# Row additions up to eight chunks ahead of their scatters, five indirect transfers under way, and gathered chunks turned sooner in the plan

## The chip, the cores and the metric

The kernel runs on one core of a Trainium2 chip. Its time is the device time of one execution in microseconds (us); the kernel before takes 2306.5 us, the median of three runs (2304.06 to 2307.6). A core has engines that run their own queues in order and wait for each other by semaphores: PE (matrix products and transposes), DVE (elementwise work, reductions and statistics), ACT (activations, copies and scalings), POOL (here the indirect transfers), and SP (here only the issue of plain transfers). Transfers of all queues are carried by 16 DMA engines.

## The reference

The input x is 32 images of 128 channels, 56 by 56 pixels (3136 tokens of 128 numbers). Cut to what matters:

```python
# layer 0: group norm, sign, a 3x3 convolution with signs as weights
x = x + conv(sign(group_norm(x)), sign(w)) * alpha
# layer 1, on tokens t = x as (image, token, channel)
n = layer_norm(t)
kv = sum over tokens of (n @ Wk + bk) * (n @ Wv + bv)
t = t + (n @ Wq + bq) * kv
# a mixture of 8 experts, the best two of each token
n = layer_norm(t)
p = softmax(n @ router_w + router_b);  top_p, top_i = top_k(p, 2);  top_p = top_p / sum(top_p)
t = t + sum over the two of top_p * (n @ expert_w[top_i] + expert_b[top_i])
```

## The kernel before

An image has 25 chunks of 128 tokens (the last of 64), in 7 blocks of four (the last of one). For each image, PE makes the convolution (`conv`, L608), DVE adds it to x (`conv_add`), PE turns chunks to tokens (`to_tokens`, L635) and ACT copies them to SBUF (`to_tokens_out`, L645, into a `tok` buffer of which there are three). DVE takes statistics, ACT scales (`scaled`), PE sums the products that give kv (`gram`), and PE projects three chunks at a time (`project`, L831), which ACT scales out of PSUM (`project_out`, L845: three multiplications and a copy) and DVE adds (`project_add`). Then DVE routes each token to two experts.

The experts are applied in two ways. The first 8 or 12 chunks of an image (`DENSE`), and all 25 of the last four images, go through all eight experts: SP loads gates spread over all partitions (`spread`, L1101, tiles `bc` and `gt`), DVE multiplies (`gated`, L1116), PE applies the experts (`experts`, L1127), DVE adds, and SP stores. The other chunks of 28 images, in four groups of 8, 8, 8 and 4 images, are sorted by the pair of experts that a token uses, 428 chunks in all:

- `row_add` (L1330, ACT) adds a number to each row of a chunk in place, and `scatter` (L1337, POOL) writes the chunk's rows by an indirect transfer to their places in a table in DRAM, `rows`.
- When all scatters of a group are through, `tile_load` (L1627, SP) loads four tiles of 128 rows at a time, `tile_turn` (PE) turns them, `tile_turned` (ACT) copies them, `tile_experts` (L1647, PE) applies two experts to each, `tile_read` (L1665, ACT) scales the results out of PSUM, two tiles a step by four activations, DVE adds (`tile_sum`, `tile_out`), and `tile_store` (SP) writes them to a table `res` in DRAM.
- When a group's `res` is complete, `gather` (L1411, POOL) fetches each chunk's rows by an indirect transfer into one of 14 `back` buffers, `back_turn` (L1424, PE) turns the gathered chunks of a block, up to four at once, which frees their buffers, `back_out` (ACT) copies them and `back_store` (SP) stores them.

A group's scatters take place while the group before is being gathered; both use POOL's queue.

**What sets the order.** The kernel is written as steps. Each step has a due time, an engine, an estimate of its work in us, the steps that it comes after, buffers of rings that it takes or frees, and a `delay` until its result has landed (`at`, L463). `in_order` (L108) walks through a model of the engines in time: of the steps that could start first on an engine, it takes the one due first, and so writes one order of all steps. A step that takes a place in a ring, such as `("sent", ...)`, waits in the plan until the step that frees the place is done. The sizes of the rings are in `ROOM` (L90): `back` has 12 places in the plan; `sent` has no buffer behind it, and only bounds how many row additions stand ahead of their scatters in the plan. None of these figures is an instruction on the chip: they change the order in which the queues of PE, DVE and ACT are written, and these three are held to the planner's order (`IN_ORDER`, L72). SP and POOL are not: the scheduler that follows arranges their instructions by its own readiness model, in an order near the planner's.

Indirect transfers have one wait of their own. `in_turn` (L1489) makes each wait for one that came some places before it in the planner's order, whether scatter or gather:

```python
before = moved[-IN_FLIGHT:][:1] if len(moved) >= IN_FLIGHT else []
for b in before:
    tc.add_manual_dep(dma.ins, b.name, in_turn_dep, reason="few under way")
```

`GATHER_LANDS` is the delay that the plan gives to a gather, so it sets how long after the gathers `back_turn` stands in PE's order. The figures beside `project_out` and `tile_read` are the plan's estimates of ACT's work.

Of the kernel before, what the change touches and what calls it, by code (L numbers as in the profile page):

```python
# [70 lines left out]

IN_ORDER = {mybir.EngineType.PE, mybir.EngineType.DVE, mybir.EngineType.Activation}  # L72
NEWTON = 3
IN_FLIGHT = 4

GATE_LANDS, SPREAD_LANDS, STORE_LANDS, TILE_LANDS, GATHER_LANDS = 5.0, 6.5, 5.0, 6.0, 12.0
TILE_PACE = (0.7, 0.6, 0.4, 0.3)
GATHER_PACE = (1.0, 0.8, 0.5, 0.4)
N_Q = C + 2 * N_EXP
# [9 lines left out]
BANKS, EMPTIES = ("ps", "acc", "ff"), 7.0  # L89
ROOM = dict(  # L90
    x=3, tok=3, ps=5, acc=1, ff=2, y=3, qs=3, tt=4, bc=4, gt=2, gated=2,
    t_in=3, turned=2, v=3, w=2, back=12, sent=4, o=2,
)


# [82 lines left out]
def conv_attn_moe_kernel(  # L178
# [32 lines left out]
    def cols_of(b):  # L211
        return blocks[b][0] * C, min(n_tok, (blocks[b][-1] + 1) * C)
# [250 lines left out]
    def at(due, key, engine, work, do, *args, after=(), take=(), free=(), delay=0.0, slack=0.0):  # L463


        if isinstance(work, float):
            steps[key] = Step(due, key, engine, work, do, args, after, take, free, delay, slack, 0.0)
            return
        running = []

        def go_on():
            if not running:
                running.append(do(*args))
            next(running[0], None)

        lag = LAG if isinstance(work, list) else 0.0
        for j, w in enumerate(work):
            last = j == len(work) - 1
            part = key if last else (*key, "part", j)
            steps[part] = Step(  # L480
                due, part, engine, w, go_on, (), [(*key, "part", j - 1)] if j else after,
                [] if j else take, free if last else [], delay if last else 0.0, slack, lag,
            )

    def base(i):

        n = len(group_of)
        return P * (min(i, n) + 1.2 * max(0, i - n))
# [42 lines left out]
    def plan_image(i: int):  # L531
        s = base(i)
# [144 lines left out]
        for g in range(n_blk):  # L677
            b = min(n_conv - 1, (cols_of(g)[1] - 1) // (ROWS * width))
            due = s + 4 + 5.5 * b
            share = len(blocks[g]) / PER  # L680
# [109 lines left out]
        for g in range(n_blk):  # L790
            share = len(blocks[g]) / PER
# [28 lines left out]
        for g in range(n_blk):  # L820
            share = len(blocks[g]) / PER
# [50 lines left out]
        for j, cs in enumerate(q_groups):  # L872
            share = len(cs) / Q_GROUP
            biased = [("bias", i, g) for g in {cs[0] // PER, cs[-1] // PER}]
            at(
                s + 85 + 3.5 * j, ("project", i, j), "PE", 0.75 * share, project, j,
                after=[("kv_8", i), ("project", i, j - 1)] + biased, take=["ps"],
                free=[("x", ("load", i))] if j == last_q else [],
            )
            at(  # L880
                s + 86 + 3.5 * j, ("project_out", i, j), "ACT", 0.92 * share, project_out, j,
                after=[("project", i, j)], take=["qs"], free=[("ps", ("project", i, j))],
            )
            at(
                s + 87 + 3.5 * j, ("project_add", i, j), "DVE", (0.58 * share,) + (0.19,) * len(cs), project_add, j,
                after=[
                    ("project_out", i, j), ("route_1", i - 2), ("row_scalars", i - 2),
                    ("var2", i - 2),
                ],
                free=[("qs", ("project_out", i, j))],  # L890
            )
# [267 lines left out]
        for b in dense_blocks:  # L1159
            share = (cols_of(b)[1] - cols_of(b)[0]) / WIDE  # L1160
# [285 lines left out]
        due = begin + each * (i - last_of[group] + GROUPS[group] - 1)  # L1446
# [6 lines left out]
        for b in range(n_dense // PER, n_blk):  # L1453
            share = len(blocks[b]) / PER
# [34 lines left out]
    def in_turn(dma):  # L1489

        before = moved[-IN_FLIGHT:][:1] if len(moved) >= IN_FLIGHT else []
        for b in before:
# [7 lines left out]
    def parts_of(g):  # L1500
        return -(-quads_of(g) * PER // C)

    def quads_of(g):
        return -(-tiles_of(g) // PER)

    def tiles_due(g):

        return base(last_of[g]) + 195, TILE_PACE[g] * P * GROUPS[g] / quads_of(g)
# [192 lines left out]
    def plan_group(g):  # L1701
        last = last_of[g]
        s = base(last)
        at(
            s + 140, ("list_1", g), "DVE", [0.2, 0.2, 0.1, 0.1, 0.1, 0.1], list_1, g,
            after=[("count_on", last), ("list_3", g - 1, parts_of(g - 1) - 1), ("pad", g - 1, 6)],
        )
        at(s + 141, ("list_sum", g), "PE", 0.2, list_sum, g, after=[("list_1", g)], take=["ps"])
        at(
            s + 142, ("list_2", g), "DVE",  # L1710
            [0.1, 0.1] + [w * parts_of(g) for w in (0.25, 0.1, 0.2, 0.2, 0.18, 0.1)], list_2, g,
            after=[("list_sum", g)], free=[("ps", ("list_sum", g))],
        )
        for h in range(parts_of(g)):
            at(
                s + 143 + h, ("list_3", g, h), "PE", 0.25, list_3, g, h,
                after=[("list_2", g), ("list_4", g, h - 1)], take=["ps"],
            )
            at(
                s + 143.5 + h, ("list_4", g, h), "DVE", 0.25, list_4, g, h,  # L1720
                after=[("list_3", g, h)] + ([("tile_experts", g - 2, quads_of(g - 2) - 1, 0)] if g > 1 else []),
                free=[("ps", ("list_3", g, h))],
            )
        for j in range(7):
            at(
                s + 143 + 3 * j, ("pad", g, j), "SP", 1.6, pad, g, 4 * j, 4 * j + 4,
                after=[("list_1", g), ("open", g), ("pad", g, j - 1)], delay=3.0,
            )
        begin, each = tiles_due(g)
        members = [i for i in group_of if group_of[i] == g]  # L1730
        for q in range(quads_of(g)):
            due = begin + each * q
            at(
                due - 12, ("tile_load", g, q), "SP", 1.4, tile_load, g, q,
                after=[("list_4", g, parts_of(g) - 1), ("pad", g, 6)]
                + [("tile_load", g, q - 1) if q else ("tile_load", g - 1, quads_of(g - 1) - 1)]
                + [("scatter", i, c) for i in members for c in range(DENSE[g], n_ck)],
                take=["t_in"], delay=TILE_LANDS,
            )
            at(  # L1740
                due, ("tile_turn", g, q), "PE", 0.45, tile_turn, g, q,
                after=[("tile_load", g, q), ("tile_turn", g, q - 1), ("tile_experts", g, q - 2, 1)],
                take=["ps"],
            )
            at(
                due + 1, ("tile_turned", g, q), "ACT", 0.47, tile_turned, g, q,
                after=[("tile_turn", g, q)], take=["turned"], free=[("ps", ("tile_turn", g, q))], slack=1.0,
            )
            for h in range(2):
                at(  # L1750
                    due + 2 + 2 * h, ("tile_experts", g, q, h), "PE", 0.90, tile_experts, g, q, h,
                    after=[("tile_turned", g, q), ("tile_experts", g, q, h - 1)], take=["ps"],
                    free=[("turned", ("tile_turned", g, q))] if h else [],
                )
                at(
                    due + 3 + 2 * h, ("tile_read", g, q, h), "ACT", 1.40, tile_read, g, q, h,
                    after=[("tile_experts", g, q, h), ("tile_read", g, q, h - 1)],
                    take=[] if h else ["v", "w"], free=[("ps", ("tile_experts", g, q, h))], slack=2.0,
                )
            at(  # L1760
                due + 9, ("tile_sum", g, q), "DVE", 0.60, tile_sum, g, q,
                after=[("tile_read", g, q, 1)], free=[("w", ("tile_read", g, q, 0))],
            )
            at(
                due + 10, ("tile_out", g, q), "DVE", 0.61, tile_out, g, q,
                after=[("tile_sum", g, q), ("tile_out", g, q - 1)],
                free=[("t_in", ("tile_load", g, q))],
            )
            at(
                due + 12, ("tile_store", g, q), "SP", 0.35, tile_store, g, q,  # L1770
                after=[("tile_out", g, q), ("tile_store", g, q - 1)]
                + ([("gather", last_of[g - 2], n_ck - 1)] if q == 0 and g > 1 else []),
                free=[("v", ("tile_read", g, q, 0))], delay=STORE_LANDS,
            )

    for i in range(n_img):
        plan_image(i)
    for g in range(len(GROUPS)):
        plan_group(g)
# [67 lines left out]
```

## Time and profile before

| | |
|---|---|
| time, median of three runs | 2306.5 us (2304.06 to 2307.6) |
| the profiled execution's own time | 2298.39 us |
| its span, first to last instruction | 2296.5 us |
| mean granted clock of PE | 0.965 |
| PE busy | 2116.7 us, 92% |
| DVE busy | 1981.4 us, 86% |
| ACT busy | 1529.2 us, 67% |
| POOL busy | 1014.6 us, 44% |
| scatters, L1339 | 428, 1174 ns each; 758.2 us idle before them |
| gathers, L1414 | 428, 1149 ns each; 501.4 us idle before them |

By the trace, the scatters of group 0 are issued from 119 to 500 us, of group 1 from 531 to 1024, of group 2 from 1037 to 1616 and of group 3 from 1636 to 1930. Gathers begin at 883 us, and the last is issued at 2280 us.

The profile is of one execution. A group's line names the source line, the engine, the operation, the tile written and the tiles read, how often, the busy time and the mean, and the idle time of the engine just before with what ended it. An idle time is put down to the semaphore that changed last before it ended, which can name an instruction that the waiting one has nothing to do with, when the wait was for several things. SPq and the like are an engine's queue. A row of the table by stretches holds, after the stretch and its length, the busy time (and instructions) of PE, PE's weight loads, DVE, ACT and POOL, then PE's granted clock as a share of full speed, the share of time in which the DMA engines were busy, and GB/s.

### The profile page before, as it was taken

Reading aid. Unit: us, or ns where it says so; the run is one execution under the profiler, and the core shown is the slowest. Engines: PE = TensorE matmul, PEld = TensorE weight load, DVE = VectorE, ACT = ScalarE, POOL = GpSimd, SP = SyncE. Lnnn points to the kernel's source line nnn. Section 1 sums busy time; section 2 is a strip of 40 time slices with the busy share of each in tenths; the row PEclk is TensorE's granted clock in tenths of the full one; section 3 lists DMA queues with packets and bytes.
Section 4 is the critical chain, followed back from the end, with each engine's and each line's share of the span. In section 5 each row is a group of like instructions: output and inputs, shape, how many; then the busy total and the mean of one; then the engine's idle time right before and its main releaser. Section 6 shows DMA issues by size and latency. Waiting matters only on the chain.

```text
span 2296.5 us, 45166 instructions
## 1 busy us (share of the span) xinstructions
PE 2116.7 (92%) x12074; PEld 1454.8 (63%) x12074; DVE 1981.4 (86%) x6370; ACT 1529.2 (67%) x4885; POOL 1014.6 (44%) x991
## 2 busy tenths in 40 slices
PE   4989999999999999898999999999789989999989
PEld 2656556566777776566767766656567765666644
DVE  4899999999999999897789899899678868778885
ACT  5767767668788987477868877455567856674311
POOL 3044434334332225544555545545545455424564
PEclk9999999999999999899999999999899989999999
DMA  4054554455555655547767866566667766877798
GB/s 168 29 162 156 167 173 145 134 182 181 189 162 179 183 186 163 162 152 247 208 198 236 250 191 216 180 209 216 208 184 219 243 186 197 259 232 239 235 298 293
DMA packets 316010, 448.56 MB, mean 195 GB/s; under 512 B 60904, under 2 KB 221200, under 8 KB 315760
## 3 DMA queue, kind: packets, MB, share of 16 engines
q1 hardware_dynamic: 286032, 382.79, 52.5%
q0 software_dynamic: 28144, 56.14, 8.0%
q10 hardware_dynamic: 1584, 6.75, 0.8%
q8 instruction: 102, 1.67, 0.3%
q14 instruction: 148, 1.21, 0.2%
HBM read 319.51 MB, written 126.00 MB: 194 GB/s over the span
## 4 chain that ended last, share of the span: by engine, by line
PE 49%; DVE 29%; DMA 7%; issue 6%; ACT 4%; SPq 2%; another core or an unknown queue 2%; POOL 1%; DVEq 0%; ACTq 0%; POOLq 0%
PE ff L1137 16%; PE cv L615 9%; PE to L1656 7%; DVE gated L1119 6%; PE gram L717 4%; PE q L836 4%; DVE st L870 3%; DVE st L655 3%; DVE tok L788 3%; DVE tok L862 2%; DMA bc<-gp 2%; DMA t_in<-rows 2%; DVE x L626 2%; PE turn L1638 2%; PE xt L642 2%
## 5 line engine op out<-in xcount | busy, mean ns | idle before, releaser
L1339 POOL DMA_INDIRECT rows<-tok,row_no x428 | 502.3, 1174 | 758.2 <-ACT tok L1333 418.4
L1137 PE MATMUL ff<-gated,ew_d 128*128 128x512 f32 (+1 forms) x1536 | 721.6, 599 | 35.0 <-DVE gated L1119 28.1
L1414 POOL DMA_INDIRECT back<-res,res_no x428 | 491.8, 1149 | 501.4 <-PE back_ps L1429 154.4
L1119 DVE TENSOR_TENSOR gated<-tt,bc 128x1024 f32<-128x1024 f32 x384 | 450.4, 1178 | 91.0 <-PE ff L1137 43.5
L1137 PEld LDWEIGHTS ff<-gated,ew_d 128*128 128x128 f32 x1536 | 277.4, 195 | 277.5 <-issue 209.9
L615 PE MATMUL cv<-xs,w_bin 128*128 128x440 bf16 (+3 forms) x2016 | 424.3, 360 | 17.9 <-ACT xs L578 10.0
L1674 ACT ACTIVATE v<-to,t_in 128x128 f32<-128x128 f32 x528 | 253.9, 481 | 129.2 <-PE to L1656 59.7
L615 PEld LDWEIGHTS <-w_bin 128*128 128x128 bf16 x2016 | 199.9, 100 | 193.4 <-issue 41.7
L850 ACT ACTIVATE qs<-q,r 128x136 f32<-128x136 f32 (+1 forms) x800 | 246.6, 407 | 63.9 <-PE q L836 36.7
L1656 PEld LDWEIGHTS to<-ew_s,turned 128*128 128x128 f32 x2112 | 258.7, 193 | 38.0 <-issue 21.9
L1656 PE MATMUL to<-ew_s,turned 128*128 x2112 | 271.3, 278 | 8.0 <-issue 2.5
L708 ACT ACTIVATE y<-tok,r 128x128 f32<-128x128 f32 (+1 forms) x800 | 253.7, 414 | 35.3 <-DVE r L522 15.2
L836 PE MATMUL q<-move,x 128*128 128x144 f32 (+1 forms) x1600 | 242.0, 298 | 11.3 <-issue 3.0
L836 PEld LDWEIGHTS q<-move,x 128*128 128x128 f32 (+1 forms) x1600 | 215.6, 195 | 42.7 <-issue 16.7
L717 PEld LDWEIGHTS gram<-y 128*128 128x128 f32 (+1 forms) x1600 | 196.7, 191 | 33.7 <-issue 23.8
L655 DVE BATCH_NORM_STATS2 st<-tok 128x6 f32<-128x128 f32 (+1 forms) x800 | 178.4, 277 | 40.6 <-ACT tok L648 33.2
L717 PE MATMUL gram<-y 128*128 128x129 f32 (+1 forms) x1600 | 208.8, 276 | 0.0
L1681 ACT ACTIVATE w<-to,t_in 128x128 f32<-128x128 f32 x528 | 206.9, 392 | 0.0
L870 DVE BATCH_NORM_STATS2 st<-tok 128x6 f32<-128x128 f32 (+1 forms) x800 | 195.0, 281 | 0.0
L626 DVE SCALAR_TENSOR_TENSOR x<-cv,alpha_col,x 128x448 f32<-128x448 f32 x224 | 151.1, 675 | 44.7 <-PE cv L615 16.7
L648 ACT COPY tok<-xt 128x512 f32<-128x512 f32 (+1 forms) x224 | 117.2, 564 | 103.5 <-PE xt L642 56.2
L1333 ACT ACTIVATE tok<-tok,a 128x128 f32<-128x128 f32 (+1 forms) x428 | 171.8, 434 | 0.2
(228 smaller groups left out, 2908.6 us busy)
## 6 DMA issues: line engine op xcount, KB each, us to landing
bc<-gp SPq DMA_DIRECT2D x368, 512.0 KB
x<-in_x_dram SPq DMA_DIRECT2D x60, 784.0 KB
t_in<-rows SPq DMA_DIRECT2D x528, 66.0 KB
res<-v SPq DMA_DIRECT2D x132, 256.0 KB
out_dram<-o SPq DMA_DIRECT2D x100, 256.0 KB
out_dram<-tt SPq DMA_DIRECT2D x92, 256.0 KB
rows<-zeros SPq DMA_DIRECT2D x116, 66.0 KB
rows<-tok,row_no POOLq DMA_INDIRECT x428
```

Source lines behind the costliest of these rows:

```text
L615: nc.tensor.matmul(cv[:, r0:r1, c0:c1], lhsT=w_bin[:, t, :], rhs=xs[:, b * ROWS + dy + r0 : b * ROWS + dy + r1, dx + c0 : dx + c1], start= ...
L655: nc.vector.bn_stats(st[:n, c, :], d["tok"][:n, c, :C])
L708: nc.scalar.mul(y[:n, j, :C], d["tok"][:n, c, :C], d["r1"][:n, c : c + 1])
L717: nc.tensor.matmul(d["gram"], lhsT=y[:n, j, :C], rhs=y[:n, j, :], start=(c == 0), stop=(c == n_ck - 1),)
L836: nc.tensor.matmul(p[:n, k, :], lhsT=d["x"][:, c * C : c * C + n], rhs=move, start=True, stop=True,)
L870: nc.vector.bn_stats(st2[:n, c, :], d["tok"][:n, c, :C])
L1119: nc.vector.tensor_tensor(g[:, :, :n], d["tt", b][:, :n].unsqueeze(1).to_broadcast([C, 2, n]), d.pop(("bc", b, k))[:, :, :n], ALU.mult,)
L1137: nc.tensor.matmul(d["ff", b][:, :n], lhsT=ew_d[:, e * C : (e + 1) * C], rhs=g[:, j, :n], start=False, stop=(e == N_EXP - 1),)
L1339: dma = nc.gpsimd.indirect_dma_start(out=groups[group]["rows"], out_offset=bass.IndirectOffsetOnAxis(ap=d["row_no"][:n, c - n_dense : c - ...
L1414: dma = nc.gpsimd.indirect_dma_start(out=d["back", c][:n, :], out_offset=None, in_=groups[group]["res"][: quads_of(group) * WIDE, :], in_o ...
L1656: nc.tensor.matmul(p[:, k, j, :], lhsT=t[:, n * C : (n + 1) * C], rhs=ew_s[:, bass.ds(d["cols", q][j][n], C)], start=True, stop=True,)
L1674: nc.scalar.activation(d["v", q][:, n, :], p[:, k, 0, :], AF.Identity, bias=row[:, C + 2 : C + 3], scale=row[:, C : C + 1],)
```

## The change

Five figures change, and nothing else. The plan lets up to eight row additions stand ahead of their scatters, where it was four. Each indirect transfer waits for the fifth before it in the planner's order, where it was the fourth. The plan takes a gather to land after 9 us, where it was 12. It takes `project_out` for three chunks to need 0.84 us of ACT, where it was 0.92, and `tile_read` 1.20 us, where it was 1.40. The second is a wait on the chip; the others alter the order in which the steps are written.

```diff
-IN_FLIGHT = 4
+IN_FLIGHT = 5
-GATE_LANDS, SPREAD_LANDS, STORE_LANDS, TILE_LANDS, GATHER_LANDS = 5.0, 6.5, 5.0, 6.0, 12.0
+GATE_LANDS, SPREAD_LANDS, STORE_LANDS, TILE_LANDS, GATHER_LANDS = 5.0, 6.5, 5.0, 6.0, 9.0
...
 ROOM = dict(
     x=3, tok=3, ps=5, acc=1, ff=2, y=3, qs=3, tt=4, bc=4, gt=2, gated=2,
-    t_in=3, turned=2, v=3, w=2, back=12, sent=4, o=2,
+    t_in=3, turned=2, v=3, w=2, back=12, sent=8, o=2,
 )
...
-                s + 86 + 3.5 * j, ("project_out", i, j), "ACT", 0.92 * share, project_out, j,
+                s + 86 + 3.5 * j, ("project_out", i, j), "ACT", 0.84 * share, project_out, j,
...
-                    due + 3 + 2 * h, ("tile_read", g, q, h), "ACT", 1.40, tile_read, g, q, h,
+                    due + 3 + 2 * h, ("tile_read", g, q, h), "ACT", 1.20, tile_read, g, q, h,
```

## The prediction

> **What bounds the kernel now.** I read the page first, then the clock and busy time by stretch, then the waits of POOL, and last the order of time around the two worst stretches. The page's first part:
>
> ```profile
> span 2296.5 us, 45166 instructions
> PE 2116.7 (92%) x12074; PEld 1454.8 (63%) x12074; DVE 1981.4 (86%) x6370; ACT 1529.2 (67%) x4885; POOL 1014.6 (44%) x991
> ```
>
> PE is idle for 2296.5 - 2116.7 = 180 us, and that is all that a change of order can win, plus what a lower clock stretches. The table by stretches (length; busy time of each engine; then PE's granted clock, the DMA share, GB/s) says where:
>
> ```profile
> 1000.00:1060.00 60.00, 49.48 (x288) 33.76 (x287) 51.97 (x192) 35.16 (x114) 33.25 (x28) 0.91 0.50 170
> 1590.00:1640.00 50.00, 35.74 (x155) 22.08 (x154) 32.01 (x114) 22.87 (x75) 25.80 (x25) 0.83 0.50 173
> 1640.00:1700.00 60.00, 57.96 (x393) 45.23 (x392) 52.67 (x145) 47.96 (x158) 26.59 (x25) 1.00 0.69 208
> ```
>
> The third row is an undisturbed stretch: PE busy 97%, clock 1.00. The first two are the ends of groups 1 and 2: PE idle 10.5 and 14.3 us, clock 0.91 and 0.83, and DVE idle too, so no engine is the bound there; a wait is. In order of time, from the answers for SP, ACT, DVE and PE (start, time taken, engine and line; in brackets the idle time before and what ended it):
>
> ```profile
> 1593.93 1.48 SPq L1110 DMA_DIRECT2D bc<-gp  x2
> 1618.69 2.81 SPq L1631 DMA_DIRECT2D t_in<-rows  x5
> 1605.79 0.40 ACT L1333 ACTIVATE tok<-tok,a 128x128 f32<-128x128 f32 x1
> 1618.81 1.56 ACT L648 COPY tok<-xt 128x512 f32<-128x512 f32 x3 [12.62 <-DMA rows<-tok,row_no]
> 1626.41 1.23 DVE L1119 TENSOR_TENSOR gated<-tt,bc 128x1024 f32<-128x1024 f32 x1 [17.96 <-DMA bc<-gp]
> 1619.45 2.18 PE L642 MATMUL xt<-ident,x 128*128 128x128 f32 x9 [10.32 <-ACT tok L648]
> 1039.93 0.59 PE L1131 MATMUL ff<-gt,eb_w 72*128 72x512 bf16 x1 [7.45 <-DMA gt<-gb]
> ```
>
> At 1594 SP reaches the first tile load of group 2, which waits for the group's last scatter, and sends nothing until 1618.69; the broadcasts (bc) queued behind it are what DVE lacks for 17.96 us. ACT stands for 12.62 us for the same scatter, since it needs its `tok` buffer, and PE stands behind ACT for 10.32 us. The last line is the same thing at group 1: PE lacks gt, which SP could not load. So I ask why the last scatters are late. POOL's queue there:
>
> ```profile
> 1603.10 0.98 POOL L1339 DMA_INDIRECT rows<-tok,row_no  x1 [0.30 <-issue]
> 1604.38 1.60 POOL L1339 DMA_INDIRECT rows<-tok,row_no  x1 [0.30 <-ACT tok L1333]
> 1608.17 0.98 POOL L1414 DMA_INDIRECT back<-res,res_no  x1 [2.19 <-PE xt L642]
> 1612.54 0.98 POOL L1414 DMA_INDIRECT back<-res,res_no  x1 [0.84 <-DMA rows<-tok,row_no]
> 1616.49 0.93 POOL L1339 DMA_INDIRECT rows<-tok,row_no  x1 [0.30 <-issue]
> ```
>
> The last row addition started at 1605.79, yet the last scatter went out at 1616.49, behind gathers that wait. They wait for a scatter issued just before them, not for the fourth before: `in_turn` counts four back in the planner's order, but only PE, DVE and ACT are held to that order, and POOL's runs otherwise. So four under way is at times one or two. From 880 to 1930, where both kinds share the queue, POOL's waits are:
>
> ```profile
> POOL rows L1339 <- ACT tok L1333: 65.0, 29, 10.8
> POOL back L1414 <- DMA rows<-tok,row_no: 51.8, 24, 6.3
> POOL back L1414 <- PE back_ps L1429: 43.7, 12, 9.7
> POOL back L1414 <- PE ff L1137: 29.7, 11, 5.4
> POOL back L1414 <- PE gram L717: 25.0, 13, 6.3
> POOL back L1414 <- DMA back<-res,res_no: 16.9, 18, 3.9
> ```
>
> A gather needs nothing of ff or gram; of PE it needs only the turn that frees its buffer. Rows put down to other PE lines are therefore, I infer, the wait for an indirect transfer too. So that wait costs POOL 51.8 + 16.9 = 69 us by the rows that name it, and 69 + 29.7 + 25.0 = 123 us or more with the misnamed.
>
> **The change, part by part.** No instruction is added or removed: the same 856 indirect transfers, 428 row additions, 428 turns. What moves is one wait, and the order.
>
> *IN_FLIGHT 4 to 5.* Each indirect transfer waits for one further back. On the path this counts only at the ends of groups. Group 2, from 1588 to 1616.5: gathers idle 5.38 + 2.16 + 2.19 + 0.84 = 10.6 us, of which 0.30 each is plain issue, so 9.4 us; the last scatter is that much sooner, SP goes on at about 1609 in place of 1618.7, and PE's 10.32 shrinks to about 1. I take 9 us of idle and 4 of the 0.17 x 50 = 8.5 us that the clock lacks in that stretch: 13. Group 1, from 988 to 1024: gathers idle 6.34 + 3.86 + 0.94 + 2.25 + 0.81 = 14.2, less 1.5 for issue = 12.7 us; the last scatter at 1024.24 comes at about 1011.5 and PE's 7.45 goes; with half of 0.09 x 60 = 5.4 us of clock, 10. Together 23. Ends: 0, if something else is late in the same place, and 10.5 + 14.3 + 5.4 + 8.5 = 39 if both stretches become like the third row. I take 23, being nearest to the rows of the gathers' idle time. What is late next is then ACT's last row addition, 1605.79, ahead of which no scatter can go.
>
> [...]
>
> *sent 4 to 8.* In the plan a row addition (ACT) may be eight scatters ahead, so it stands earlier in ACT's order. Before 880 POOL carries scatters alone and waits 353 of its 418 us for row additions there, with nobody behind it but the end of group 0, where SP loses about 6 us under a DVE that is 97% busy: 0. From 880 to 1930 the row is 65.0 us in 29 waits; on the path it moves the 1605.79 above, four additions or so earlier. This could turn group 2's 13 into 18; it is within the 39, and I add 0. Its cost: 4 more additions, each 0.30 from start to next start, may stand in front of ACT work that PE waits for: 1.2 us per image, 28 images, 34 us at the most and 0 if ACT has slack. ACT is 67% busy, so I take 0, and keep 34 for the rivals.
>
> *GATHER_LANDS 12 to 9.* The turns (PE) stand up to 3 us earlier. PE's idle time put down to gathered chunks is 0.5 us in all 428, so there is room; POOL stands 154 us for buffers that turns free, of it 110.6 after 1930, when no scatter is behind. Cost 0, bounds -2 and +6 (the two turns that waited, each 3 us later).
>
> *0.92 to 0.84 and 1.40 to 1.20.* These are costs in the plan, not on the chip. ACT's order of time shows what they should be:
>
> ```profile
> 600.61 0.46 ACT L1674 ACTIVATE v<-to,t_in 128x128 f32<-128x128 f32 x1 [0.39 <-PE to L1656]
> 601.81 0.41 ACT L1333 ACTIVATE tok<-tok,a 128x128 f32<-128x128 f32 x1
> ```
>
> A `tile_read` takes 1.20 from its start to the next step's; a full `project_out` 0.83 (1595.07 to 1595.90). The plan gets truer by 264 x 0.20 + 32 x 8.3 x 0.08 = 74 us of ACT, but loses what had been slack: PE steps that take ACT's results stand closer behind. The nearest rows are PE's waits on ACT, 11.9 (xt for tok), 10.0 (cv for xs), 6.7 (cv for tok), 2.3 and 2.0 (q): 33 us, 10 of them counted above. All 23 gone, or doubled, are the ends; I take a loss of 3, because every new order has a stall or two of its own.
>
> Sum: -23 + 3 = -20 us. The profiled execution took 2298.4 with a span of 2296.5 (1.9 lie around it), and would take 2278; the median of the three runs is 8.1 above it, 2306.5, so I forecast 2286.5.
>
> [...]
>
> **The rivals.**
> *The wait only changes its name* (14%). The last scatters come sooner, but the planner puts SP's tile load sooner as well, and SP stands as long. For it: SP's place follows the same plan. Against it: at 1605.79 to 1616.49 it is POOL, not the plan, that is late. Then 23 goes and the 3 stays at most: 2306 +- 4.
> *Row additions crowd ACT* (18%, slower). Place: ACT's queue just ahead of `xt_out` and `tt_out`, which PE waits for. Price: 34 us if all 28 images pay, and PE's clock with it. Against the 20 won, it decides from about 17 images, or from half of them where the gain is only partly there. For it: from 504 to 864 ACT is busy for 57 to 64 of every 72 us. Against: PE waits for tok only 18.6 us now. At the full price: 2286.5 + 34 = 2320.
> *A fifth transfer under way slows SP's broadcasts* (6%, slower). Place: 1930 to the end, at a DMA share of 0.80. Price: DVE waits for bc 32.1 us in 11 waits over the span, 14 without the 17.96 counted; tripled, and PE behind each, that adds 28 us: 2315. It decides from 20 us more, 2.4 times the 14. For it: the share. Against: POOL's stream there stands for turned buffers (110.6 us), so a fifth is rarely under way.
>
> **How the numbers follow.** The forecast has 62%; 2286.5, with a range of its own of 2272 to 2300. Of the 14% of the renamed wait, 10 fall within 0.2% (4.6 us, about what a measurement of this kernel can tell), 2 on each side. Faster 0.62 + 0.02 = 0.64, same 0.10, slower 0.18 + 0.06 + 0.02 = 0.26. The range goes down to the forecast less the rest of the bound, 2286.5 - (39 - 23) - 6 = 2264, and up to the crowded ACT's 2320; a tenth lies beyond at each end.
>
> **What would show it.** Right: the rows of POOL back behind DMA rows and DMA back shrink from 69 us to under 30; SP's gap before the first tile load of groups 1 and 2 falls from 21 and 23 us to under 15; DVE's wait of 17.96 and PE's of 10.32 and 7.45 are gone or halved; no clock under 0.9 in those stretches; PE still waits under 2 us for gathers. Wrong: SP's gaps as long as before, PE's waits on ACT (33 us) well up, or new PE idle over 5 us at the end of group 3, or where images 25 to 31 are started.

## The result, and the profile after

The changed kernel takes 2400.7 us, the median of four runs (2395.7 to 2406.5), where the kernel before takes 2307.1 (2304.1 to 2310.9). The ratio is 1.0387, with an interval of 1.0354 to 1.0421: 3.9% slower, where 2286.5 and a gain were forecast. Later sets of runs gave something that no line of the first two traces had told: the kernel before takes about 2300 us in some sets and about 2235 in others, and the change is slower in the first and faster in the second. The text calls them the first and the second condition. The result belongs to the first.

The first part of the page of the changed kernel, as shown of before:

```profile
span 2393.6 us, 45129 instructions
PE 2136.3 (89%) x12074; PEld 1475.5 (62%) x12074; DVE 1987.4 (83%) x6370; ACT 1527.2 (64%) x4885; POOL 1002.3 (42%) x991
```

The work is the same and PE's idle time is up from 180 to 257 us. It is not lost where the forecast looked. In the table by stretches (length; busy time of PE, PE's weight loads, DVE, ACT and POOL; PE's clock, DMA share, GB/s) the first 500 us, before any tile is read or chunk gathered, have PE busy for 422 us, 15 less than before (436.75), and DVE for 426 (448.27 before):

```profile
0.00:500.00 500.00, 422.18 (x2328) 276.88 (x2329) 425.95 (x1561) 312.65 (x1012) 160.04 (x258) 0.94 0.40 133
```

The first tile load of the four groups starts 27, 51, 81 and 85 us later than before (534.4, 1078.6, 1699.7 and 2016.7), the end 97 us: the loss grows evenly. The end of group 2, from the answers for ACT, POOL, SP, DVE and PE in order of time, with the idle time before in brackets:

```profile
1673.92 0.32 SPq L1110 DMA_DIRECT2D bc<-gp  x1
1696.71 0.46 ACT L1333 ACTIVATE tok<-tok,a 128x128 f32<-128x128 f32 x1
1697.14 1.28 POOL L1339 DMA_INDIRECT rows<-tok,row_no  x1 [0.30 <-issue]
1699.70 0.90 SPq L1631 DMA_DIRECT2D t_in<-rows  x2
1719.15 1.23 DVE L1119 TENSOR_TENSOR gated<-tt,bc 128x1024 f32<-128x1024 f32 x1 [19.84 <-DMA bc<-gp]
1720.43 2.07 PE L1137 MATMUL ff<-gated,ew_d 128*128 128x512 f32 x2 [10.15 <-DVE gated L1119]
```

The wait that the change was to remove is gone: the last scatter leaves 0.4 us after the last row addition (10.7 us before, 1605.79 to 1616.49). But the addition itself is late, SP still sends nothing for 25.5 us (1674.24 to 1699.70; 23.3 before), and DVE and PE stand as long as before.

The list of waits shows rows that are new or changed (us, times, longest):

```profile
ACT v L1674 <- remote: 62.8, 9, 12.8
ACT qs L850 <- remote: 25.9, 8, 8.1
POOL back L1414 <- DMA rows<-tok,row_no: 33.8, 14, 5.3
PE cv L615 <- ACT xs L578: 26.6, 6, 6.9
```

"Remote" means that the semaphore changed, and that no instruction on record that updates it had ended in the 1.5 us before. Before, the first row was 19.3 us, the second 2.4 and the third 51.8. PE's wait for `xs` was 10.0. One of them in full, from the answers for PE, ACT and POOL of the changed kernel:

```profile
341.01 3.73 PE L836 MATMUL q<-move,x 128*128 128x144 f32 x26
345.72 0.72 ACT L1333 ACTIVATE tok<-tok,a 128x128 f32<-128x128 f32 x2
347.60 0.96 POOL L1339 DMA_INDIRECT rows<-tok,row_no  x1 [0.30 <-issue]
348.86 1.14 POOL L1339 DMA_INDIRECT rows<-tok,row_no  x1 [0.30 <-issue]
349.95 0.90 ACT L850 ACTIVATE qs<-q,r 128x136 f32<-128x136 f32 x3 [3.51 <-remote]
351.54 0.86 PE L615 MATMUL cv<-xs,w_bin 128*128 128x448 bf16 x2 [6.80 <-ACT xs L578]
```

PE's projections end at 344.74. ACT's `project_out` waits for three of them, which the trace ends at 343.61, and for a DVE step that frees its buffer and ended at 344.98, and yet it starts at 349.95; PE then lacks the `xs` that ACT makes next. All the while POOL issues scatters back to back, one each 1.26 us. The profile's own legend says that the ends of matmuls are modelled, and all that this trace holds of the wait is those ends and the later change of the semaphore. So a single wait can't tell whether the product or the message is late; the text says that the result is late.

I counted them: each wait of ACT or DVE for PE's semaphore and nothing else, with the engine idle over 0.15 us before it. A wait that a separate instruction makes just before counts as the engine's too, so the place above, with its wait for DVE, isn't among them. The semaphore's value in the program names the matmul that must end; a result is late when the start comes over 1 us after that matmul's recorded end. Sorted by how many indirect transfers POOL had issued back to back, with less than 0.4 us between two, when the matmul ended (late, of all such waits):

| kernel and condition | none | 1 or 2 | 3 or 4 | 5 to 8 | 9 and more | late in all |
|---|---|---|---|---|---|---|
| before, first | 0 of 123 | 10 of 64 | 28 of 65 | 14 of 24 | 3 of 3 | 55 |
| after, first | 0 of 122 | 12 of 56 | 44 of 78 | 29 of 38 | 5 of 6 | 90 |
| before, second | 0 of 130 | 0 of 66 | 0 of 50 | 0 of 17 | 0 of 3 | 0 |
| after, second | 0 of 112 | 0 of 42 | 0 of 45 | 0 of 26 | 0 of 11 | 0 |

The expectations below count more loosely: they leave out a wait made just before, so some of their late starts waited for something else. Counted so there are 122 and 167 in the first condition (73 and 111 of them with over 1 us of idle time), and 31 and 23 in the second.

In the first condition no result is late in these two traces while POOL issues nothing (in its other seven, at most 5 of 120), and the share of late results grows with the run to 76% at five to eight. In the second condition all 502 starts come within 0.07 us of the recorded end, so the modelled ends serve here. PE itself is not held: in 54 of the 55 and 87 of the 90 cases it had, by its records, begun later matmuls before the waiting engine started. `sent` = 8 lets ACT prepare more scatters, so POOL's runs of eight and more go from 9 to 35 (the expectation's 39 is an earlier count). The other engines' results show nothing of it: DVE's start ACT and PE within 0.06 us in all four traces; ACT's start DVE within 0.04 us, and PE over 1 us late 8 and 5 times in the first condition, 7 and 5 in the second.

### The profile page after: what moved, and what is told of

Same layout as the page of the kernel before. It is cut to its first block, busy times and chain, and to the rows that moved or that the text cites. A ratio compares the mean times of both kernels' runs of the same rounds, so it can differ in the third digit from the quotient of the medians.

```text
span 2393.6 us, 45129 instructions
## 1 busy us (share of the span) xinstructions
PE 2136.3 (89%) x12074; PEld 1475.5 (62%) x12074; DVE 1987.4 (83%) x6370; ACT 1527.2 (64%) x4885; POOL 1002.3 (42%) x991
## 4 chain that ended last, share of the span: by engine, by line
PE 64%; DVE 17%; ACT 5%; issue 4%; DMA 4%; another core or an unknown queue 3%; SPq 1%; ACTq 0%; DVEq 0%
PE ff L1137 19%; PE cv L615 13%; PE to L1656 8%; PE q L836 6%; PE gram L717 6%; DVE gated L1119 4%; PE xt L642 3%; PE turn L1638 2%; DMA bc<-gp 2%; DVE tok L788 2%; DVE st L870 2%; DVE st L655 1%; DVE tok L862 1%; PE back_ps L1429 1%
## 5 line engine op out<-in xcount | busy, mean ns | idle before, releaser
L1339 POOL DMA_INDIRECT rows<-tok,row_no x428 | 486.3, 1136 | 826.0 <-ACT tok L1333 421.2
L1137 PE MATMUL ff<-gated,ew_d 128*128 128x512 f32 (+1 forms) x1536 | 713.3, 593 | 36.4 <-DVE gated L1119 34.6
L615 PE MATMUL cv<-xs,w_bin 128*128 128x440 bf16 (+3 forms) x2016 | 431.0, 363 | 33.1 <-ACT xs L578 26.6
L1656 PEld LDWEIGHTS to<-ew_s,turned 128*128 128x128 f32 x2112 | 266.7, 198 | 56.0 <-issue 33.4
L1656 PE MATMUL to<-ew_s,turned 128*128 x2112 | 279.5, 284 | 22.2 <-issue 11.0
L836 PE MATMUL q<-move,x 128*128 128x144 f32 (+1 forms) x1600 | 253.7, 308 | 30.0 <-issue 13.4
L836 PEld LDWEIGHTS q<-move,x 128*128 128x128 f32 (+1 forms) x1600 | 225.5, 203 | 63.0 <-issue 33.8
L862 DVE TENSOR_TENSOR tok<-tok,qs 128x384 f32<-128x384 f32 (+1 forms) x288 | 149.0, 517 | 33.5 <-ACT qs L850 19.3
```

Source lines behind the costliest of these rows:

```text
L615: nc.tensor.matmul(cv[:, r0:r1, c0:c1], lhsT=w_bin[:, t, :], rhs=xs[:, b * ROWS + dy + r0 : b * ROWS + dy + r1, dx + c0 : dx + c1], start= ...
L836: nc.tensor.matmul(p[:n, k, :], lhsT=d["x"][:, c * C : c * C + n], rhs=move, start=True, stop=True,)
L1137: nc.tensor.matmul(d["ff", b][:, :n], lhsT=ew_d[:, e * C : (e + 1) * C], rhs=g[:, j, :n], start=False, stop=(e == N_EXP - 1),)
L1339: dma = nc.gpsimd.indirect_dma_start(out=groups[group]["rows"], out_offset=bass.IndirectOffsetOnAxis(ap=d["row_no"][:n, c - n_dense : c - ...
L1656: nc.tensor.matmul(p[:, k, j, :], lhsT=t[:, n * C : (n + 1) * C], rhs=ew_s[:, bass.ds(d["cols", q][j][n], C)], start=True, stop=True,)
```

## The experiments

**The edits one by one.** Each is the kernel before with one line of the diff.

```
e1: ("project_out", i, j), "ACT", 0.84 * share     e2: ("tile_read", g, q, h), "ACT", 1.20
e3: sent=8                                          e4: IN_FLIGHT = 5
```

> Of the five edits only the planned cost of project_out, 0.92 to 0.84. Theory B (bursts): with sent = 8 GpSimd issues scatters eight and more back to back (39 bursts of 8 or more after the change, 9 before), and while it does, ScalarE and VectorE get TensorE's results late; then this edit alone makes 2306 +- 12. Theory A (tight plan): the planner puts ACT's steps closer to PE's than the chip can follow, and the two plan costs carry the loss of 94 us; then this edit alone makes 2335 or more. Theory D (any new order costs): every edit alone is 10 to 40 us slower and none carries half.

> Of the five edits only the planned cost of tile_read, 1.40 to 1.20. Theory B (bursts): 2306 +- 12. Theory A (tight plan): 2330 or more, the loss after 504 us alone, since no tile is read sooner. Theory D: 10 to 40 us slower.

> Of the five edits only sent, 4 to 8. Theory B (bursts): 2370 to 2400, 30 or more bursts of eight or more scatters, and the first tile load of group 0 about 20 us later than 507. Theory A (tight plan): within 15 us of 2306. Theory D: 10 to 40 us slower. The prediction on record had 0 for this edit.

> Of the five edits only IN_FLIGHT, 4 to 5. The prediction on record had 23 us of gain, 2283. Theory B (bursts): the wait four back breaks bursts too, so some loss may come with it, but less than a third of the 94: 2285 to 2335. Theory A: 2283 to 2306. Theory D: 10 to 40 us slower.

The kernel before took 2233.9 us here (28 runs), so this set fell in the second condition. Ratios: e1 1.0006 (0.999 to 1.002), e2 0.9956 (0.993 to 0.998), e3 0.9943 (0.991 to 0.998), e4 0.9983 (0.996 to 1.001). No theory had it: nothing is slower. The bursts are there in e3 (25 runs of eight and more) and cost nothing; no result is late. That made the condition itself the question.

**The two kernels again, and the change less one part.** `r_before` and `r_after` are the two kernels as they are; e7 is the changed kernel with `sent` = 4, e6 with the costs 0.92 and 1.40.

> The kernel before, unchanged, for a trace from the chip that ran the four single edits, where it took 2233.9 us and not 2307. Theory C (chip): on the first chip TensorE's results reached ScalarE and VectorE late (73 waits that ended over 1 us after the matmul's end in the trace, 185 us of idle in all); on this chip at most 25 such waits. Theory M (one kernel, one time): 2300 us and as many late waits as in the first trace.

> The changed kernel, unchanged, beside the kernel before on one chip. Theory C (chip): the loss of 94 us belongs to the late results, of which the new order meets more (111 against 73); on a chip without them it is 2215 to 2240 against 2234. Theory M: the change is 3.9% slower on any chip, by the five edits together, though each alone was between 0.994 and 1.001.

> All edits but sent, which stays 4. Theory C: 2215 to 2240, as the change itself. Theory M with the bursts as cause: the loss is gone here, and r_after has it. Theory M with the tight plan as cause: as slow as r_after.

> All edits but the two planned costs, which stay 0.92 and 1.40. Theory C: 2210 to 2235. Theory M with the tight plan as cause: the loss is gone here and r_after has it; with the bursts as cause: as slow as r_after.

The kernel before took 2233.2 us, the second condition; in its trace no result is late (by the expectation's count 11, not 73). The change: 2204.9 us, ratio 0.9867 (0.983 to 0.990), a gain of 28 us. e7: 0.9948 (0.993 to 0.997). e6: 0.9899 (0.986 to 0.994). So the kernel that is 3.9% slower in one condition is 1.3% faster in the other, and the single edits nearly add up: -13 for `sent`, -10 for `tile_read`, -4 for `IN_FLIGHT`, +1 for `project_out`. The place shown above, in the same program, from the answers of r_after for PE, ACT and POOL:

```profile
326.79 2.13 PE L836 MATMUL q<-move,x 128*128 128x144 f32 x14 [0.36 <-ACT qs L854]
329.22 0.73 ACT L1333 ACTIVATE tok<-tok,a 128x128 f32<-128x128 f32 x2
329.25 0.96 POOL L1339 DMA_INDIRECT rows<-tok,row_no  x1 [0.30 <-issue]
329.81 0.92 ACT L850 ACTIVATE qs<-q,r 128x136 f32<-128x136 f32 x3
331.42 1.92 PE L615 MATMUL cv<-xs,w_bin 128*128 128x448 bf16 x8 [2.51 <-ACT xs L578]
```

POOL issues as densely (a scatter each 1.26 us from 326.72 to 331.77), and ACT goes from the row additions into `project_out` without a wait. The order is good; it is the late result that makes it bad.

What IN_FLIGHT does alone is seen at the end of group 2 in e4 (answers for ACT and POOL):

```profile
1568.25 0.40 ACT L1333 ACTIVATE tok<-tok,a 128x128 f32<-128x128 f32 x1
1572.05 0.92 POOL L1339 DMA_INDIRECT rows<-tok,row_no  x1 [0.30 <-issue]
```

In r_before the same two are at 1564.55 and 1575.16: the gap shrank from 10.6 to 3.8 us, but the new order has the last row addition 3.7 us later, so the group ends 3.1 us sooner, not 9. In r_after, with all five edits and no late result, the last scatter follows its row addition by 0.4 us, and SP still sends nothing for 25.5 us (1530.61 to 1556.12; 23.2 in r_before), and DVE stands 15.6 us (17.9). So that stall belongs to the new order, not to late results.

**The last single edit, the change with IN_FLIGHT = 4 or 2, and a later landing in the plan.**

```
e5: GATHER_LANDS = 9.0 alone                 e8: the changed kernel, IN_FLIGHT = 4
e9: the changed kernel, IN_FLIGHT = 2        e10: the changed kernel, ("scatter", i, c) ... delay=12.0
```

> Of the five edits only GATHER_LANDS, 12 to 9. Theory S (the edits add up on the two later chips: -14 for sent, -5 for IN_FLIGHT, -8 for tile_read, +2 for project_out, -28 for all): what is left for this edit is -3, so a ratio of 0.996 to 1.001. The prediction on record had 0, bounds -2 and +6. Theory R (late results grow with GpSimd's runs): if the kernel before takes about 2307 here as on the first chip, still within 10 us of it, since no scatter moves.

> All edits but IN_FLIGHT, which stays 4. Theory S: 5 us slower than the whole change, a ratio of 0.989. The prediction on record had the whole gain in IN_FLIGHT, so a ratio of 1.001 here. Theory R, only on a chip where the kernel before takes about 2307: nearly as slow as the whole change there, 1.02 or more, since sent = 8 makes the long runs.

> The changed kernel with IN_FLIGHT = 2, so that GpSimd issues fewer indirect transfers back to back. On a chip as the two later ones: GpSimd's runs fall from 41 of eight or more to under 10, nothing is gained by it, and the waits of gathers for transfers cost 0 to 60 us: a ratio of 0.987 to 1.015. Theory R on a chip where the kernel before takes about 2307: under 40 late results, and faster than the kernel before there, 0.97 to 0.99. If late results don't follow the runs, it is 1.03 or more there.

> The changed kernel, and in the plan a scatter takes 12 us to land, not 3. The stall at the end of group 2 (VectorE waits 15.6 us for its broadcast, which SP holds behind the first tile load) is left on every chip. If the plan's early tile load makes it, it shrinks to under 6 us and the ratio is 0.98 to 0.987; if not, it is 0.987 to 1.0.

The kernel before took 2305.5 us: the first condition. e5: 1.0020 (0.998 to 1.006), 64 late results. e8: 1.0275 (1.019 to 1.036), 82 late; the loss is mostly there without a fifth transfer. e10: 1.0274 (1.021 to 1.034), 89 late. In e10 SP's gap at the end of group 2 fell from 25.5 to 10.9 us and DVE's longest wait for `bc` from 19.8 to 4.1, and most of the loss stayed: the end of a group isn't what it is about. e9 went against its expectation, 1.0768 (1.071 to 1.083), though the late results fell to 3 (43 by the expectation's count, which had under 40), with no run of POOL longer than five. Its list of waits says why:

```profile
POOL rows L1339 <- DMA rows<-tok,row_no: 170.6, 64, 6.0
PE back_ps L1429 <- DMA back<-res,res_no: 153.3, 60, 10.7
```

With two under way each transfer waits for the landing of another, and PE, which before had no wait for gathers, stands 153 us for them. This bought fewer late results with a dearer wait, and left open whether the runs are the cause. (The expectation's 41 runs of eight and more are 36, counted again.)

**A pause after each indirect transfer.** It keeps the order of PE, DVE, ACT and SP, and POOL's but for eight gathers that change places with a scatter; it keeps the depth, and takes the density away. The write goes to a tile that nothing reads.

```
+    pause = const.tile([C, 384], mybir.dt.uint8, name="pause")
...
         moved.append(dma.ins)
+        step = nc.gpsimd.memset(pause, 0)
+        tc.add_manual_dep(step.ins, dma.ins.name, order_only, reason="a pause")
```

> The changed kernel with one write of 128x384 bytes on GpSimd after each of the 856 indirect transfers (estimate from the rows of other writes there: 0.3 to 0.6 us each), which changes no result. Theory R (GpSimd's runs without a gap make TensorE's results late): where the kernel before takes 2306, late results fall from 167 to under 80 of all waits and the ratio from 1.039 to under 1.01. If the runs only go with the lateness, it stays at 1.03 or more, and the pauses cost extra. Where the kernel before takes 2234: 0.985 to 1.0 by both.

> Only sent, 4 to 8, again. Theory R where the kernel before takes 2306: 1.02 to 1.03, since all edits but IN_FLIGHT made 1.0275 there and GATHER_LANDS 1.002. If the two plan costs make the loss instead, it is within 0.5% there. Where the kernel before takes 2234: 0.994 again.

> All edits but sent, which stays 4, again. Theory R where the kernel before takes 2306: 1.00 to 1.015, IN_FLIGHT's share of the longer runs. If the two plan costs make the loss: 1.025 or more. Where the kernel before takes 2234: 0.995 again.

The kernel before took 2297.3 us, the first condition again. e11 takes 2248.1 us: a ratio of 0.9782 (0.973 to 0.984), where the change without the pause has 1.0387. The late results fell from 90 to 6. POOL's queue in e11:

```profile
334.80 0.44 POOL L1499 MEMSET pause<- 128x384 uint8 x1
335.41 0.97 POOL L1339 DMA_INDIRECT rows<-tok,row_no  x1 [0.17 <-ACT xs L578]
336.38 0.43 POOL L1499 MEMSET pause<- 128x384 uint8 x1
```

At its densest POOL now issues a transfer each 1.58 us (334.80 to 336.38 is one round), not each 1.26. The pauses add 371 us of work to POOL, and the kernel is still some 6% faster than the change alone, by the two ratios; the changed kernel without the pause wasn't in this set. The runs cause the loss: the late results and the time go when the density of the issues is taken away. The other two runs of the set: `sent` alone (e12) 1.0121 (1.006 to 1.019), 68 late, less than the expected 1.02; all but `sent` (e13) 0.9980 (0.995 to 1.001), 47 late, just under the expected 1.00 to 1.015. So `sent` makes the loss, and the other edits deepen it (1.012 to 1.039) but make none without it. Which of them deepens it wasn't tried further; IN_FLIGHT seems part of it (1.0275 without, from another set).

Ordered by late results, the kernels of the first condition are ordered by time too, but for two that tie: 6 (0.978), 47 (0.998), 55 (1), 64 (1.002), 68 (1.012), 82 (1.0275), 89 (1.0274), 90 (1.039). Only e9, with its own wait, stands outside.

**The pause without the change, and side by side.**

> The kernel before with the pause after each indirect transfer. Theory R where the kernel before takes about 2300: the 123 late results of before go too, so a ratio of 0.97 to 0.99; the change is then worth about 1% with the pause on both. If the pause only mends what the change broke: 0.995 to 1.01. Where the kernel before takes 2234: 0.995 to 1.01.

> The changed kernel again. Where the kernel before takes about 2300: a ratio of 1.03 to 1.04. Where it takes 2234: 0.987.

> The changed kernel with the pause, again, beside e15. Where the kernel before takes about 2300: 0.975 to 0.985. Where it takes 2234 there are few late results to save, and the pause costs GpSimd 0.33 us per transfer: 0.985 to 1.0.

The kernel before took 2240.0 us: the second condition. e14 (before, with the pause): 1.0147 (1.010 to 1.019), 36 us slower. e15 (the change): 0.9853 (0.982 to 0.989). e16 (the change with the pause): 1.0030 (1.001 to 1.005), 39 us slower than e15. So here, with no late result to save, the pause only costs, and more than the expectations had. What it does for the kernel before in the first condition wasn't run. The changed kernel with the pause takes 2248 us in the first condition and 2245 in the second: it is the fastest where the kernel before takes 2300, and the changed kernel alone, with 2205, where that takes 2235. Set side by side, five programs tell what the first condition costs each, by the medians: 3 us for the change with the pause (6 late results there), 68 for all but `sent` (47), 57 to 73 for the kernel before (55), 106 for `sent` alone (68) and 196 for the change (90).

## Why the prediction was wrong

*What failed.* The step "sent 4 to 8", with "so I take 0" at its end. It looked for the cost of early row additions in ACT's queue, and for what stands behind POOL. It held POOL's own stream to be free, "with nobody behind it but the end of group 0". In the condition of the result that stream makes PE's results late, 55 in the kernel before and 90 after, and denser scatters make it worse: `sent` alone costs 1.2% there, 28 us, and all five edits 94. The trace of before had the sign of it, `v` behind "remote" for 19.3 us; the working didn't ask what such a row was.

*IN_FLIGHT, -23.* The wait was read rightly, and it went: 0.4 us in place of 10.7. The size was wrong. In the second condition the edit alone gains 4 us (0.9983): ACT's last row addition, which the text named as "what is late next", was set later by the new order. With all five edits SP stands 25.5 us there in both conditions, so the order, not late results, uses the gain up. IN_FLIGHT alone wasn't run in the first condition.

*GATHER_LANDS, 0.* Right: 1.002 with an interval around 1, in the first condition, the only one in which it ran alone.

*The plan's costs, +3.* In the second condition -9: `project_out` +1, `tile_read` -10. That a truer plan places ACT's steps better, by more than a new order stalls, is a likely reason, but no run shows it. In the first, all edits but `sent` together give 0.998.

*The sum, -20.* In the second condition the change gains 28 to 33 us, so the sum was near, but by other terms: `sent` and `tile_read` in place of IN_FLIGHT. Sum and sign are wrong in the first.

*The rivals.* "Row additions crowd ACT" had the right edit and the right sign. Its mechanism isn't it: PE's waits for `xs` are up from 10.0 to 26.6 us, but ACT stands idle ahead of them, waiting for PE, and the same order costs 13.9 in the second condition. Its price, 34 us, was a third of the loss, so the range ended at 2320. "The wait only changes its name" is right for SP, which stood 25.5 us at the end of group 2, in r_after too, and wrong in its price, 2306 +- 4. "A fifth transfer slows SP's broadcasts" isn't seen: the DMA share is 0.78 after 2000, and SP's broadcasts cost DVE 35.1 us in place of 32.1. Nor does the DMA share tell the two conditions apart: in the first 500 us it is 0.45 in r_after, more than the 0.40 of the slower run.

```profile
0.00:500.00 500.00, 437.27 (x2439) 286.58 (x2440) 450.40 (x1670) 329.18 (x1074) 180.56 (x271) 0.96 0.45 145
```

*The signs named ahead.* Right: PE still waits under 2 us for gathers, and POOL's gathers wait less for transfers, though not under 30 us: 33.8 + 7.3 = 41 over the whole span, where before has 51.8 + 29.1 = 81 (69 of it from 880 to 1930). Wrong, as named: SP's gap at the end of group 2 as long as before (25.5 us; 16.7 in place of 21.5 at group 1, where under 15 was named), and PE's waits on ACT well up (86 us in all, 46 before).

## What to carry to other kernels

A wait put down to "remote", or one that ends microseconds after its releaser, is a question to settle before any sum is made: take the matmul that the semaphore belongs to, and see what else was running while its result was under way. A queue that seems to have slack set another engine's pace here by how densely it issued (in the first condition 90 late results of PE with a transfer of POOL each 1.26 us at the densest, 6 with one each 1.58), so an edit that lets one engine run further ahead is costed by that too. And a ratio of two kernels measured in one set of runs need not hold in the next: here the same two programs differ by +3.9% and by -1.3%.

## What was not expected of the hardware

- The kernel before takes 2307, 2305 and 2297 us in three sets of runs and 2234, 2233 and 2240 in the other three. The lists of results number the chip: number 9 had 2234 in one set and 2305 in another, so the number alone doesn't tell the condition. What makes the condition stays open.
- In the first condition a result of PE reaches ACT or DVE over 1 us late in none of 245 waits of the two first traces when POOL issues no indirect transfer, and in 43% to 76% of them after three to eight back to back. A pause of 0.43 us on POOL between transfers takes most of it away (6 late in place of 90). By what path POOL's transfers hold PE's results is open.
- The condition can be read from a trace in one more way. In the first it holds 2651 of the 3210 semaphore updates that PE's matmuls make (before), 2759 of 3247 (after); in the second 3193 and 3211. The loss is not PE's alone: before, the first holds 3761 of DVE's 4896 and 2374 of ACT's 3098, though none of DVE's results is late. Why these records are missing is not shown, nor whether the late results have the same cause; e11 speaks against a plain link: with 2438 of 3247 it lost the most and had only 6 late results. Every run here was traced, so none tells what an untraced run takes.
